# Moving the maxima's subtraction, delta*x and the values' products in a planned attention, routing and scan kernel

## The chip, the cores and the metric

One core of one Trainium2 chip runs the whole kernel. The time is device microseconds for one execution, the median of the runs shown; a profiled execution, taken apart from these, gives the trace.

## The reference, cut to what matters

Sixteen independent sequences of 512 tokens and 256 features (B, T, D = 16, 512, 256) in float32 pass through four blocks. Each block adds its result to x.

```python
def attn_a(x):                       # on layernorm(x)
    xn = x * rsqrt(mean(x * x) + EPS) * norm_w
    q, k, v = heads(xn @ Wq.T + bq), heads(xn @ Wk.T + bk), heads(xn @ Wv.T + bv)   # 16 heads of 16
    scores = where(causal, -inf, q @ k.T / 4)
    out = softmax(scores) @ v
    return xn + out @ Wo.T + bo

def attn_b(x):                       # selective scan with 16 states, on layernorm(x)
    xc = silu(conv4(x) + conv_b)
    delta = softplus(xc @ Wd.T + bd)
    Bm, Cm = xc @ Wb.T, xc @ Wc.T
    h = exp(A * delta) * h + delta * xc * Bm     # for each feature and state, step by step over T
    y = sum_over_states(h * Cm)
    return (y * sigmoid(x @ Wg.T + bg)) @ Wo.T + bo

def ffn(x):                          # base product, a shared low rank and 2 of 6 routed low ranks
    return base(x) + shared(x) + sum(top2_weight * routed(x))

x = x + attn_a(layernorm(x)); x = x + ffn(layernorm(x))
x = x + attn_b(layernorm(x)); x = x + ffn(layernorm(x))
```

## The kernel before, in words

**The plan.** The loop over the 16 sequences (L886) doesn't issue instructions. It records operations with `op(engine, cost, function, r=, w=, ...)` (L84): an engine, an estimated duration, the buffers read and written, and further buffers that have to be free at its start (`also`). `Plan.order` (L126) then plays the whole list through a small model of the engines: at each moment a free engine takes, among its ready operations whose buffers are free, the one with the smallest due time. The due time is `STARTS[sequence] + TURNS[place in the sequence]` (L130), two tables of numbers written out in the file. For ScalarE, `CHANGE` is added to the due time of an operation that needs another activation table than the loaded one (L149). While a score product waits for its reader, `kept` reserves the reader's engine (and TensorE afterwards), so that a filler is taken only if it ends at most `OVER` after the reserved moment (L151 to L154). The order that comes out is the order of the instructions in each engine's queue, and an engine works its queue in order; the waits on the chip are real semaphores, so a wrong estimate can only make an engine stand still. For a DMA, the model takes its issue (0.65 or 0.7 us), then a share of one common link (`load`, 2.3 us for a scan load) and 2.0 us until it has landed.

**Buffers.** `sizes` (L415) gives the number of each: 4 of x (so at most four sequences are under way), 3 of qT, 4 of kT, 2 of qm, one each of pt0 to pt3, 5 of dd. In PSUM there are one buffer `sc` of four banks for scores and four single banks `one`.

**Attention** (L538). Tokens are normalised and transposed into xtA. Heads come in four groups j of four; two groups make a pair i. For a pair one product gives the queries of 8 heads, each in 16 of 128 rows; two ScalarE passes (L626) write it to two tiles qT, in each of which every second block of 16 rows is scaled to zero, so that each head of a group has a block of 32 rows of which 16 are zero. kT is made in the same way, with a 1 in the first row of the zero half (bk with first_row added). Then:

- for each query tile t of 128 tokens and each group, `four` (L560) runs four score products (one per head, 32 rows of the array each, L566) and four products with identb and a mask (full array, L568) into sc, and VectorE takes the negated row maximum (L637) into negm;
- negm is transposed on TensorE (L645); the maximum of a head then lies in the first of the zero rows of that head;
- VectorE adds this row to the queries: qm = one * first_row + qT (L650), one for each group of the pair. With the 1 in kT, the score product then contains the maximum's subtraction;
- `weights_values` (L575): for each key tile kt, `four` gives the transposed scores in sc, ScalarE exponentiates them into pt (L585), and four products `weigh` (L590; tiles of 128 rows and 32 columns, one per head) accumulate values and the row sum over kt in one bank. Each of the four weigh steps is an operation of its own. The sums are copied (L596), transposed (L601) and divided (L608, L609).

Then the heads' outputs are transposed and projected (L662 to L671).

**Scan** (L766). After convolution and gates, delta (dt, L812) and delta*x (dx, which takes a buffer of tag sg, L817, on VectorE) are stored to DRAM in rows (L816, L819), and read back with each row spread over 16 partitions (dd, L849, two DMAs of 512 KB for each of 16 dd tiles of a sequence). GpSimd multiplies by B (L856), ScalarE makes the decays in a bank (L861), VectorE scans (L864), GpSimd multiplies by C (L867), and TensorE sums over the states with ysel (L874, again tiles of 128 rows and 32 columns). All DMAs of a sequence are issued by SyncE, in planned order. In the model, operations with `port=True` (GpSimd's and L817) exclude each other.

**Routing** (L674) is run after attention and after the scan: low-rank products (L687), the top two of six by small VectorE operations, one transposition (L754) and the projection.

`project` (L515) ends each block: products into a bank, then VectorE adds it to x (L528).

## Time and profile before

| | |
|---|---|
| median of 3 runs | 2063.27 us (2061.38 to 2065.82) |
| the profiled execution's own time | 2066.51 us |
| its span, first to last instruction | 2064.7 us |
| mean granted TensorE clock | 0.954 |
| instructions | 34733 |
| scans, L864 on DVE | 512 x 1212 ns |
| products by B and C, L856 and L867 on POOL | 256 x 2361 and 256 x 2358 ns |
| row maxima, L637 on DVE | 256 x 1486 ns (684 to 2285) |
| exponentials, L585 on ACT | 256 x 1235 ns (594 to 1872) |
| moved by DMA | 316 MB, 153 GB/s over the span |

How to read it. The page gives the busy time of each engine, then 40 slices of the span with a digit for tenths of busy time. A group line has the line of the code, the engine, the operation, output and inputs, shapes and count; then busy time and mean of one; then the idle time of the engine just ahead of it and what ended it. In a timeline a line is a run of like instructions: start, duration, engine, line, operation, and in brackets a wait ahead of it. A float32 product counts as two TensorE instructions, so that a step of four products appears as x8. Ends of products are modelled and overlap the next start. PEld is the load of weights. The x16 of the DMA issues to L889 and L894 are the loads and stores of the 16 sequences.

### The profile page before, as it was taken

Reading aid. Unit: us, or ns where it says so; the run is one execution under the profiler, and the core shown is the slowest. Engines: PE = TensorE matmul, PEld = TensorE weight load, DVE = VectorE, ACT = ScalarE, POOL = GpSimd, SP = SyncE. Lnnn points to the kernel's source line nnn. Section 1 sums busy time; section 2 is a strip of 40 time slices with the busy share of each in tenths; the row PEclk is TensorE's granted clock in tenths of the full one; section 3 lists DMA queues with packets and bytes.
Section 4 is the critical chain, followed back from the end, with each engine's and each line's share of the span. In section 5 each row is a group of like instructions: output and inputs, shape, how many; then the busy total and the mean of one; then the engine's idle time right before and its main releaser. Section 6 shows DMA issues by size and latency. Waiting matters only on the chain. (4 is left out here: it accounts for less than half of the span.)

```text
span 2064.7 us, 34733 instructions
## 1 busy us (share of the span) xinstructions
PE 1801.9 (87%) x13253; PEld 953.8 (46%) x13253; DVE 1513.4 (73%) x2479; ACT 1194.0 (58%) x1685; POOL 1371.1 (66%) x814
## 2 busy tenths in 40 slices
PE   4788789999999999999999999999999999996455
PEld 2244344555455454545455454545554454544123
DVE  4335677878788787878788787878788787876563
ACT  2236556565666757565666667575666766564431
POOL 3001784949587685859597785859596785848693
PEclk8789899999999999999999999999999999998766
DMA  3000956848494866847494867849493957747791
GB/s 93 1 1 22 216 122 155 197 127 210 109 233 109 216 164 167 205 137 191 110 231 100 225 153 175 204 120 212 110 231 95 228 143 186 183 125 183 186 222 31
DMA packets 113064, 316.35 MB, mean 153 GB/s; under 512 B 17809, under 2 KB 36610, under 8 KB 112898
## 3 DMA queue, kind: packets, MB, share of 16 engines
q1 hardware_dynamic: 112194, 313.99, 62.5%
q8 instruction: 105, 1.72, 0.4%
q14 instruction: 61, 0.50, 0.1%
q10 hardware_dynamic: 704, 0.14, 0.0%
HBM read 287.87 MB, written 26.21 MB: 152 GB/s over the span
## 5 line engine op out<-in xcount | busy, mean ns | idle before, releaser
L864 DVE TENSOR_TENSOR_SCAN dd<-one,dd 128x512 f32<-128x512 f32 x512 | 607.9, 1212 | 185.2 <-ACT one L861 88.3
L856 POOL TENSOR_TENSOR dd<-dd,bc 128x1024 f32<-128x1024 f32 x256 | 603.6, 2361 | 194.0 <-DMA dd<-drows 156.8
L867 POOL TENSOR_TENSOR dd<-dd,bc 128x1024 f32<-128x1024 f32 x256 | 601.9, 2358 | 86.2 <-DVE dd L864 80.4
L637 DVE TENSOR_REDUCE negm<-sc 128x4 f32<-128x512 f32 (+3 forms) x256 | 380.4, 1486 | 154.0 <-PE sc L568 153.7
L861 ACT ACTIVATE one<-dd,am 128x512 f32<-128x512 f32 x512 | 344.3, 689 | 249.4 <-DVE dd L864 108.9
L585 ACT ACTIVATE pt<-sc 128x2048 f32<-128x2048 f32 (+3 forms) x256 | 316.3, 1235 | 189.0 <-PE sc L568 187.8
L487 POOL TENSOR_SCALAR rs<-mv 128x4 f32<-128x4 f32 x64 | 12.3, 193 | 364.2 <-DVE mv L482 361.4
L566 PE MATMUL sc<-qm,kT 32*128 32x512 f32 (+3 forms) x2048 | 214.1, 488 | 37.8 <-ACT pt L585 28.4
L566 PE MATMUL sc<-kT,qT 32*128 32x128 f32 (+3 forms) x2048 | 217.0, 494 | 30.5 <-DVE negm L637 25.9
L568 PEld LDWEIGHTS <-identb 128*128 128x128 bf16 x2048 | 117.4, 98 | 232.4 <-issue 217.2
L874 PE MATMUL one<-dd,ysel 128*32 128x512 f32 x1024 | 172.7, 633 | 55.5 <-POOL dd L867 46.4
L590 PE MATMUL one<-pt,vv 128*32 128x512 f32 (+3 forms) x2048 | 191.6, 449 | 8.1 <-DVE dd L864 7.9
L566 PEld LDWEIGHTS sc<-qm,kT 32*128 32x128 f32 x2048 | 80.9, 185 | 181.5 <-ACT pt L585 120.4
L474 PE MATMUL one<-base,xtR 128*128 128x256 f32 x512 | 139.5, 395 | 18.6 <-DVE dd L864 18.0
L566 PEld LDWEIGHTS sc<-kT,qT 32*128 32x128 f32 x2048 | 82.0, 187 | 156.8 <-DVE negm L637 63.3
L494 ACT ACTIVATE xhR<-x,nm,rs 128x256 f32<-128x256 f32 x192 | 99.4, 588 | 53.2 <-POOL nm L490 53.1
L528 DVE TENSOR_TENSOR x<-one,x 128x512 f32<-128x512 f32 x128 | 86.4, 675 | 34.7 <-PE one L474 34.5
L474 PEld LDWEIGHTS one<-base,xtR 128*128 128x128 f32 x512 | 94.5, 194 | 36.8 <-DVE dd L864 21.5
L481 DVE BATCH_NORM_STATS2 st<-x 128x6 f32<-128x256 f32 x256 | 103.7, 405 | 4.8 <-DMA x<-in_x_dram 4.1
L568 PE MATMUL sc<-mask_q,identb 128*128 128x128 bf16 x1024 | 103.7, 225 | 0.0
L568 PE MATMUL sc<-mask_k,identb 128*128 128x128 bf16 x1024 | 102.8, 224 | 0.0
L505 PE MATMUL one<-ident,xhR 128*128 128x128 f32 x384 | 61.9, 290 | 35.2 <-ACT xhR L494 27.7
(132 smaller groups left out, 2449.4 us busy)
## 6 DMA issues: line engine op xcount, KB each, us to landing
dd<-drows SPq DMA_DIRECT2D x512, 512.0 KB
x<-in_x_dram SPq DMA_DIRECT2D x16, 512.0 KB
drows<-dt SPq DMA_DIRECT2D x32, 256.0 KB
drows<-sg SPq DMA_DIRECT2D x32, 256.0 KB
bc<-brows SPq DMA_DIRECT2D x16, 512.0 KB
out_dram<-x SPq DMA_DIRECT2D x16, 512.0 KB
brows<-few SPq DMA_DIRECT2D x16, 64.0 KB
wo<-in_Wo_dram SPq DMA_DIRECT2D x2, 256.0 KB
```

The source lines that it names most:

```text
L474: nc.tensor.matmul(o[:, lo:hi], lhsT=lhsT, rhs=rhs, start=n == 0, stop=n == len(todo) - 1)
L481: nc.vector.bn_stats(st()[:, t, :], x()[:, t, :])
L566: nc.tensor.matmul(sc()[:, g, 0:n], lhsT=lhsT(g), rhs=rhs(g), start=True, stop=False)
L568: nc.tensor.matmul(sc()[:, g, at : at + P], lhsT=identb, rhs=mask, start=False, stop=True)
L585: o.then = op("ACT", act(G * n), lambda pt=pt, sc=sc, n=n: nc.scalar.activation(pt(), sc()[:, :, 0:n], AF.Exp), r=[sc], w=[pt], table="exp")
L590: nc.tensor.matmul(av()[rows(g), kt * P : T], lhsT=vals()[:, kt, G * j + g, :], rhs=pt()[:, g, :], start=kt == 0, stop=kt == NT - 1,)
L637: o.then = op("DVE", dve(G * n), lambda t=t, n=n, sc=sc, nm=nm, s=s: nc.vector.tensor_reduce(nm()[:, t, :, 1 - s, 0:1], sc()[:, :, 0:n], A ...
L856: op("POOL", pool(1024), lambda dd=dd: nc.gpsimd.tensor_tensor(dd()[:, :, 1, :], dd()[:, :, 1, :], both(0), ALU.mult), port=True, r=[(bc, ...
L861: op("ACT", act(512) + 0.07, lambda i=i, k=k, dd=dd, dec=dec: nc.scalar.activation(dec(), dd()[:, i, 0, :], AF.Exp, scale=am[:, k + 4 * i ...
L864: op("DVE", 1.22, lambda i=i, dd=dd, dec=dec: nc.vector.tensor_tensor_scan(dd()[:, i, 1, :], dec(), dd()[:, i, 1, :], 0.0, ALU.mult, ALU.a ...
L867: op("POOL", pool(1024), lambda dd=dd: nc.gpsimd.tensor_tensor(dd()[:, :, 1, :], dd()[:, :, 1, :], both(1), ALU.mult), port=True, r=[(bc, ...
L874: nc.tensor.matmul(sums()[rows(g), :], lhsT=ysel[:, m, :], rhs=four[g]()[:, g % 2, 1, :], start=m == 0, stop=m == 3)
```

## The change

- The row maxima: the transposed negm is copied by ScalarE to a new tile nT (one buffer), and for each group of the pair one DMA on SyncE's queue copies its four rows (2 KB each) from nT into the first zero rows of qT, in place. The two VectorE operations into qm and the qm buffers are gone; qT has 4 buffers in place of 3, and stays in use until the last score product of its group.
- `weigh` is one operation for each group, behind its four exponentials: 16 products in one run, four key tiles one after the other. It reads pt0 to pt3 and is marked `mode="columns"`, as L874's sum is; in the model an operation of TensorE costs 0.2 us less behind one of the same mode.
- delta*x is computed by GpSimd in place of VectorE.
- The plan: estimates of several operations, OVER, CHANGE and both tables of due times have new values; a sequence has 366 operations in place of 376.

```diff
-OVER, CHANGE = 2.3, 97.0
+OVER, CHANGE = 2.5, 0.0
 STARTS = (
-    0, 149, 234, 338, 413, 521, 619, 700, 790, 888, 996, 1074, 1174, 1263, 1369, 1447,
+    0, 332, 605, 865, 1160, 1414, 1634, 1884, 2099, 2343, 2583, 2879, 3172, 3456, 3728, 3999,
 )
...
+                if eng == "PE":
+                    cost -= 0.2 * (o.mode is not None and o.mode == mode)
+                    mode = o.mode
...
-        "hT": (2, [NU + 1, T]), "qT": (3, [P, T]), "kT": (4, [P, T]), "qm": (2, [P, T]), "avs": (2, [P, T]),
+        "hT": (2, [NU + 1, T]), "qT": (4, [P, T]), "kT": (4, [P, T]), "nT": (1, [P, T]), "avs": (2, [P, T]),
...
     def act(n):
-        return 0.2 + n / 1200.0
+        return 0.17 + n / 1200.0
...
-            o = op("PE", pe(n, 1, 0.09) + 0.45, run, r=reads, w=[sc], also=[into])
+            o = op("PE", pe(n, 1, 0.0) + 0.5, run, r=reads, w=[sc], also=[into])
...
             av, avs = psum("one"), sbuf("avs")
+            pts = [sbuf(f"pt{kt}") for kt in range(NT)]
             for kt in range(NT):
                 n = T - kt * P
-                pt = sbuf(f"pt{kt}")
+                pt = pts[kt]
...
-                def weigh(kt=kt, pt=pt, av=av, j=j):
+            def weigh():
+                for kt in range(NT):
                     for g in range(G):
                         nc.tensor.matmul(
-                            av()[rows(g), kt * P : T], lhsT=vals()[:, kt, G * j + g, :], rhs=pt()[:, g, :],
+                            av()[rows(g), kt * P : T], lhsT=vals()[:, kt, G * j + g, :], rhs=pts[kt]()[:, g, :],
                             start=kt == 0, stop=kt == NT - 1,
                         )
 
-                op("PE", pe(n, 1, 0.1), weigh, r=[pt, vals], w=[av], also=[avs])
+            op("PE", 2.2 + 0.2, weigh, r=pts + [vals], w=[av], also=[avs], mode="columns")
...
-            qms = [sbuf("qm"), sbuf("qm")]
-            op("PE", 0.66, turn, r=[nm], w=[one], also=qms)
-            for s, qm in enumerate(qms):
-                op("DVE", dve(512) + 0.06, lambda qm=qm, one=one, qT=pairs[s][0], s=s: nc.vector.scalar_tensor_tensor(
-                    qm(), one(), first_row[:, 1 - s : 2 - s], qT(), ALU.mult, ALU.add
-                ), r=[one, pairs[s][0]], w=[qm])
-            for s in range(2):
-                weights_values(2 * i + s, pairs[s][1], qms[s])
+            nT = sbuf("nT")
+            op("PE", 0.57, turn, r=[nm], w=[one], also=[nT])
+            op("ACT", act(512), lambda nT=nT, one=one: nc.scalar.copy(nT(), one()), r=[one], w=[nT])
+            for s, (qT, kT) in enumerate(pairs):
+                row = slice(HD * (1 - s), P, 32)
+                op("SP", 0.65, lambda nT=nT, qT=qT, row=row: nc.sync.dma_start(out=qT()[row, :], in_=nT()[row, :]),
+                   r=[nT], w=[qT], load=0.1)
+            for s, (qT, kT) in enumerate(pairs):
+                weights_values(2 * i + s, kT, qT)
...
-            op("DVE", dve(512) + 0.1, lambda e=e: nc.vector.tensor_tensor(dx()[:, e, :], dt()[:, e, :], xc()[:, e, :], ALU.mult),
+            op("POOL", pool(512), lambda e=e: nc.gpsimd.tensor_tensor(dx()[:, e, :], dt()[:, e, :], xc()[:, e, :], ALU.mult),
                r=[(dt, e), (xc, e)], w=[(dx, e)], port=True)
...
-                op("PE", pe(512, 1, 0.18), add, r=[four[0], four[2]], w=[sums])
+                op("PE", pe(512, 1, 0.18), add, r=[four[0], four[2]], w=[sums], mode="columns")
```

The due times (TURNS) are replaced throughout and left out here. Other estimates that change: a step of four transpositions 0.66 to 0.57, the division 0.72 to 0.68, the routing's small VectorE steps by 0.08 to 0.2 each, the values' products less 0.2.

## The prediction

> **What bounds the kernel now.** I read five views: the busy shares and slices of the page, the stretches, SyncE's timeline (for the rhythm), TensorE's timeline (for what one step costs there), and the groups by shape (for durations).
>
> ```profile
> PE 1801.9 (87%) x13253; PEld 953.8 (46%) x13253; DVE 1513.4 (73%) x2479; ACT 1194.0 (58%) x1685; POOL 1371.1 (66%) x814
> PE   4788789999999999999999999999999999996455
> ```
>
> ```profile
> 155.00:1858.00 1703.00, 1584.71 (x12054) 841.64 (x12056) 1347.02 (x2182) 1077.01 (x1518) 1208.48 (x702) 0.99 0.67 164
> 1858.00:2064.00 206.00, 111.70 (x468) 60.09 (x468) 112.61 (x184) 71.75 (x110) 145.45 (x77) 0.73 0.66 156
> ```
>
> The columns after the length are PE, PEld, DVE, ACT and POOL busy, then PE's clock and the DMA share. PE is at 9 tenths in nearly every slice between a head and a tail: 93% from 155 to 1858 us, 54% in the last 206 us. In the middle DVE has 79%, POOL 71%, ACT 63% and the DMA engines 67%. PE's own timeline lists 112 us of waits in that stretch, 6.6%. So the middle is PE's, taken in order; the tail is latency, with POOL the busiest.
>
> SyncE's timeline (start, duration) gives the rhythm:
>
> ```profile
> 1092.38 0.54 SPq L894 DMA_DIRECT2D out_dram<-x  x1
> 1102.95 0.39 SPq L889 DMA_DIRECT2D x<-in_x_dram  x1
> 1207.93 0.55 SPq L894 DMA_DIRECT2D out_dram<-x  x1
> 1219.17 0.38 SPq L889 DMA_DIRECT2D x<-in_x_dram  x1
> 1323.70 0.55 SPq L894 DMA_DIRECT2D out_dram<-x  x1
> ```
>
> The first sequence is stored at 399.8 us, then one every 115.5 us until 1785.8 (12 periods, 1386 us), then three in the last 275 us. A period holds 115.5 x 0.066 = 7.6 us of PE waits and 107.9 us of PE work.
>
> What does a weighting step (L590) cost on PE? Its timeline tells if starts are compared:
>
> ```profile
> 998.27 0.50 PE L566 MATMUL sc<-qm,kT 32*128 32x128 f32 x8
> 998.71 0.40 PE L568 MATMUL sc<-mask_k,identb 128*128 128x128 bf16 x4
> 999.04 1.07 PE L590 MATMUL one<-pt,vv 128*32 128x512 f32 x8
> 1000.03 0.71 PE L566 MATMUL sc<-qm,kT 32*128 32x256 f32 x8
> 1000.68 0.40 PE L568 MATMUL sc<-mask_k,identb 128*128 128x128 bf16 x4
> 1001.01 0.85 PE L590 MATMUL one<-pt,vv 128*32 128x384 f32 x8
> 1001.68 1.04 PE L874 MATMUL one<-dd,ysel 128*32 128x512 f32 x8
> 1002.65 0.50 PE L566 MATMUL sc<-kT,qT 32*128 32x128 f32 x8
> 1003.08 0.40 PE L568 MATMUL sc<-mask_q,identb 128*128 128x128 bf16 x4
> 1003.41 0.64 PE L590 MATMUL one<-pt,vv 128*32 128x256 f32 x8
> 1003.98 0.66 PE L601 MATMUL one<-ident,avs 128*128 128x128 f32 x4
> ```
>
> Modelled ends overlap, so I take start to next start. The 384-wide step before L874, also in 128x32 tiles, takes 0.67 us; its others before a full-array product take 0.78 (median). The 256-wide one takes 0.46 before L874, 0.57 before a full-array product (here), 0.76 before scores. With no change of tile shape I get 0.25, 0.46, 0.67 and 0.88 us for 128 to 512 columns (the 0.25 and 0.88 by the 0.21 per 128 columns): 2.26 us for four. Leaving column tiles adds 0.11 to 0.30. Entering them adds 0.10: the four mask products last 0.33 us before L590 and 0.23 before a full-array product, over 300 cases.
>
> **What the Trainium skill says.** "TensorEngine Tiling (Array Packing)", section Tiling Modes, says that changing the tiling mode drains TensorE; the 0.10 and 0.11 to 0.30 us above agree. "DMA: Bandwidth & Descriptors", section Why a DMA increments its semaphore by 16 and not by 1, says that a transfer runs on the largest number of engines up to 16 that divides its slowest dimension, the lowest-numbered ones: the new transfers have 4 rows, so 4 engines, on the queue that carries the scan's loads. No such shape is in the trace. "SBUF — State Buffer", section Who interferes with whom, says that a VectorE operation with two SBUF inputs and a GpSimd one exclude each other; L817 (two SBUF inputs) takes 809 ns, the same shape from PSUM (L880) 685, which fits. "ScalarE: Activation LUTs", What ACT_TABLE_LOAD costs, gives 1283 ns; the trace has 1283, 68 times.
>
> **The change, part by part.**
>
> ```profile
> L650 DVE SCALAR_TENSOR_TENSOR qm<-one,first_row,qT 128x512 f32<-128x512 f32 x64 | 44.8, 741 | 12.4 <-PE one L645 12.4
> L817 DVE TENSOR_TENSOR sg<-dt,xc 128x512 f32<-128x512 f32 x32 | 25.9, 809 | 8.6 <-ACT dt L812 8.6
> L856 POOL TENSOR_TENSOR dd<-dd,bc 128x1024 f32<-128x1024 f32 x256 | 603.6, 2361 | 194.0 <-DMA dd<-drows 156.8
> ```
>
> 1. Values' products in one run. Between 155 and 1858 us there are 222 steps, 4 to a group of heads. About half are followed by scores, a third by full-array products, 39 by L874 (no change). Weighted with the medians (0.12 after 512 and 384 before scores, 0.30 after 256, 0.11 before full arrays) the exits come to 27.9 us, 0.50 per group of heads; 221 of 222 are entered from a full array, 0.10 each, 0.40 per group. One run pays one exit (0.11 to 0.30) and one entry: 0.25 to 0.40 in place of 0.90, so 0.50 to 0.65 us less; I take 0.65. Four groups: **2.6 us of PE per period**, 41.6 us over 64 groups. Against it: four score weights (pt0 to pt3, one buffer each) stay taken until the run is over, so the next group's first score product waits for about 2.3 us more. The score buffer sc is held per group for 8.7 us of PE (3.02 of scores and 1.32 of masks, twice), 10.9 us of reductions and exponentials and some 3 us of handing over, 22.5 of the 28.9 us that a quarter period has: 6.4 us are spare. I take zero; if that cover is gone it costs up to 2.3 x 4 = 9.2 us a period.
>
> 2. Maxima by ScalarE and transfers. Removed: 64 of L650, 44.8 us of DVE, 3.0 a period. Added: 32 ScalarE copies like L596 (583 ns), 18.7 us, on an engine with 63%; 64 SyncE issues at 0.33 us (the issue of the small store L829), 21 us; 64 transfers of 8 KB, little beside 512 KB each for the scan. Path from the transposed maxima to the first score product: before 2 x 0.74 = 1.5 us on DVE for both heads; after 0.58 + 2 x 0.33 + a landing. Nearest for the landing: from the store of few (1021.02) to the load that waits for it (1022.74), 1.7 us. So 2.9 us in place of 1.5: 1.4 later, twice a period, hidden where PE has products of three other sequences in between. Upper end: behind ten of the scan's loads at 2.16 us each (62.5% of the span over some 600 loads' worth of bytes), 21.6 us. Lower end: below nothing, since DVE's own queue no longer delays it. I take zero. Behind a waiting transfer on SyncE stand the scan's loads, for which POOL L856 waits; behind a waiting score product stands all of PE.
>
> 3. Delta*x on GpSimd. DVE loses 25.9 us, 1.6 a period. POOL gains 32 at half of L856 plus something, 1.2 us: 38 us, 2.4 a period, on 71%. Each of the two is 0.4 us later for its store, and may stand behind one 2.36 us product; POOL is mostly idle there, since the scan has not begun. Zero.
>
> 4. Order. Costs, due times (STARTS, TURNS), OVER and CHANGE all change, so every queue is laid out anew. CHANGE 0 takes away the preference for the loaded ScalarE table: between none and 8 more loads of 1.28 us a period (six activations alone among exponentials would need 12 where 4.25 are now). The trace bounds this to 0 to 10 us of ScalarE a period; I take zero, as ScalarE has 37% free.
>
> Sum: 12 periods x 2.6 = 31 us; of the other 16 groups (head and tail, PE half busy) half of 16 x 0.65, 5 us. PE waits behind the scan on DVE for 43 us in the middle (L474, L645, L505, L590 by L864); with 4.6 of 91 us less on DVE I count nothing. The profiled run is 2066.5 us (span 2064.7 and 1.8 around it): 2066.5 - 36 = 2030.5. It lies 3.2 above the median of the runs, so **2027 us**, 1.7% faster. Next late is still PE, with 112.9 a period.
>
> **Rivals.**
> More gain: the waits of 43 us behind DVE's scan go too, and POOL and DVE no longer exclude each other at delta*x: 2027 - 43 = 1984. For it: DVE is second at 79%. Against: those waits are for PSUM buffers, not for DVE's load.
> No gain: an x buffer comes free only with a store, and the next load follows it by 10 us; if the 450 us that a sequence stays set the period, PE's gain is idle time: 2063. Against: a sequence's own chain (attention 90 us of sc, scan 75 us of POOL) is much shorter.
> **Slower**: the small transfers arrive later than the fixed order of PE assumes. The place is the first score product of a pair of head groups, twice a period; PE stops there with all that is queued behind. It decides from 1.3 us of lateness each (2 x 1.3 = 2.6). Behind one or two of the scan's loads, 3 us each, it costs 12 x (6 - 2.6) = 41 us: 2104. With the pt buffers' 9.2 us a period in full it would be 12 x 6.6 = 79: 2142. For it: SyncE's queue is in order, and it waits 715 us in all for scan buffers to come free (dd by L874). Against: the order counts 2 us and the load of the link for each transfer.
> That it doesn't do what it says: the runs of four may stand where a switch is needed anyway, and the due times may undo the rest; 2060.
>
> **How the numbers follow.** Forecast 0.40 (2005 to 2055, own range), more gain 0.15, no gain 0.08, slower 0.35, not as said 0.02. About 0.2% (4 us) is what a measurement of this kernel can tell from no change. Faster: 0.40 + 0.15 + 0.03 of the two weak cases; same 0.07; slower 0.35. The range leaves out some 0.07 of the strong gain below 1988 and 0.13 of the losses above 2100.
>
> **What would show it.** Right: a store every 112 to 113 us, L590 some 10% shorter in sum, PE above 92% in the middle. Wrong: PE waiting at L566 for a transfer into qT, waits at sc for pt, table loads far above 68, DMA waits at L856 grown, or a longer tail.

## The result and the profile after

| | before | after |
|---|---|---|
| median of the runs made side by side | 2064.55 us (4 runs) | 2146.77 us (2144.03 to 2156.54, 4 runs) |
| ratio, 95% interval | | 1.0409 (1.0372 to 1.0446) |
| the profiled execution | 2066.51 us | 2144.24 us |
| its span | 2064.7 us | 2142.4 us |
| mean granted TensorE clock | 0.954 | 0.918 |

The kernel became slower, by 82 us where 36 us less was forecast, and it lies above the range. In the page of the kernel after, these are TensorE's busy share and its slices, with the granted clock in tenths:

```profile
PE 1827.1 (85%) x13253; PEld 982.5 (46%) x13253; DVE 1445.5 (67%) x2383; ACT 1208.2 (56%) x1719; POOL 1410.8 (66%) x846
...
PE   5778789998989989899989999899989999987445
...
PEclk8679899999999999999999999999999999988657
```

TensorE has the same 13253 products and is busy for 25 us longer, although one run of the values' products was to save time. SyncE's timeline of the kernel after, with the stores (L903) and loads (L898) of x:

```profile
984.00 0.39 SPq L903 DMA_DIRECT2D out_dram<-x  x1
988.70 0.39 SPq L898 DMA_DIRECT2D x<-in_x_dram  x1
...
1103.47 0.39 SPq L903 DMA_DIRECT2D out_dram<-x  x1
1107.58 0.54 SPq L898 DMA_DIRECT2D x<-in_x_dram  x1
```

A store comes every 119.5 us here, in place of 115.5; over 12 periods the mean is 119.8. The load of B and C for the scan (bc), one for each sequence, gives a cleaner sum of the 78 us: the first comes at 222 us in place of 205 (+17), the 15 intervals after it have 119.6 in place of 115.8 (+57), and from the last to the end there are 126.7 us in place of 122.2 (+4). So most of the loss, 57 of the 78 us, is in the rhythm. The first scan's later start was not looked into.

What TensorE waits for, of the kernel before (total us, times, longest):

```profile
PE one L874 <- POOL dd L867: 46.4, 28, 7.2
PE sc L566 <- ACT pt L585: 32.7, 83, 2.0
PE one L505 <- ACT xhR L494: 27.7, 7, 10.7
PE sc L566 <- DVE negm L637: 26.3, 22, 2.4
```

and of the kernel after:

```profile
PE sc L570 <- ACT pt L590: 115.1, 101, 3.3
PE one L883 <- POOL dd L876: 65.5, 36, 12.0
PE sc L570 <- DVE negm L644: 45.1, 46, 3.7
```

The wait of a score product for the exponentials that read the score buffer before it has grown by 82 us. That this is as much as the loss is chance: the period has 4.3 us of it (below), beside other changes. No line of TensorE's products has a transfer into qT. To see where that wait stands, TensorE's timeline of the kernel after:

```profile
959.44 0.93 PE L570 MATMUL sc<-qT,kT 32*128 32x384 f32 x8
960.30 0.40 PE L572 MATMUL sc<-mask_k,identb 128*128 128x128 bf16 x4
962.23 0.50 PE L570 MATMUL sc<-qT,kT 32*128 32x128 f32 x8 [1.54 <-ACT pt L590]
962.67 0.40 PE L572 MATMUL sc<-mask_k,identb 128*128 128x128 bf16 x4
963.75 1.24 PE L570 MATMUL sc<-qT,kT 32*128 32x256 f32 x8 [0.69 <-ACT pt L590]
964.92 0.61 PE L572 MATMUL sc<-mask_k,identb 128*128 128x128 bf16 x4
966.64 2.09 PE L570 MATMUL sc<-kT,qT 32*128 32x512 f32 x8 [1.11 <-ACT pt L590]
968.66 0.61 PE L572 MATMUL sc<-mask_q,identb 128*128 128x128 bf16 x4
969.20 3.00 PE L597 MATMUL one<-pt,vv 128*32 128x512 f32 x32
```

Four score steps follow one another with nothing but waits between them, and the run of 32 (L597, the values' products) stands behind all four. In the timeline of the kernel before, the weigh steps and other products stand between such steps. The durations tell a second thing: from 963.75 on the score step of 256 columns takes 1.24 us, the one of 512 takes 2.09, where the prediction's lines have 0.71 for 256, and 1.14 (at 955.99 in the kernel after) is normal for 512. The stretches of the kernel after (PEclk is the third figure from the end) say why:

```profile
957.00:964.00 7.00, 4.62 (x52) 3.38 (x52) 4.04 (x13) 6.02 (x8) 3.93 (x2) 0.98 1.04 233
964.00:971.00 7.00, 5.89 (x36) 1.99 (x40) 5.45 (x12) 3.30 (x5) 7.00 (x4) 0.53 1.05 233
971.00:1077.00 106.00, 99.41 (x759) 54.63 (x752) 80.16 (x123) 66.00 (x97) 76.96 (x48) 1.00 0.64 156
```

After a stretch in which TensorE was busy for 4.6 of 7 us, its clock is halved for some 7 us, once a period; the same happens at 844 us. In the kernel before no record between 303 and 1883 us has a lowered clock. The Trainium skill, "TensorE: Matmul & The Clock Gate", section A second HAM failure mode: psum-queue depth-cycling, says that frequent short idle times between groups of products can make the clock go back and forth between half and full; this trace agrees, with waits of at most 1.54 us in the stretch ahead.

To compare kernels below, I add up TensorE's timeline between the stores of the first and the thirteenth sequence, by start to next start less the waits, and divide by 12. "Work" is all of it, "weigh" the values' products, "for pt" the waits of a score product for exponentials; "half clock" is the time for which the clock records have half speed there.

| us a period | period | work | of it weigh | waits | of them for pt | half clock |
|---|---|---|---|---|---|---|
| before | 115.5 | 109.1 | 11.4 | 6.3 | 1.4 | 0 |
| after | 119.8 | 109.9 | 10.0 | 9.9 | 5.7 | 7.7 |

### The profile page after: what moved, and what is told of

Its sections match the earlier page's. It is cut to its first block, busy times and chain, and to the rows that moved or that the text cites. A ratio compares the mean times of both kernels' runs of the same rounds, so it can differ in the third digit from the quotient of the medians.

```text
span 2142.4 us, 34874 instructions
## 1 busy us (share of the span) xinstructions
PE 1827.1 (85%) x13253; PEld 982.5 (46%) x13253; DVE 1445.5 (67%) x2383; ACT 1208.2 (56%) x1719; POOL 1410.8 (66%) x846
## 4 chain that ended last, share of the span: by engine, by line
PE 55%; POOL 13%; DVE 12%; ACT 10%; issue 4%; DMA 4%; SPq 0%; POOLq 0%; ACTq 0%; DVEq 0%
PE one L478 21%; PE sc L570 13%; PE one L597 7%; POOL dd L876 6%; PE sc L572 6%; ACT pt L590 5%; PE one L883 4%; DVE dd L873 4%; DMA dd<-drows 4%; DVE negm L644 3%; POOL dd L865 3%; POOL rs L492 2%; ACT xhR L498 2%; PE one L509 1%; DVE st L485 1%
## 5 line engine op out<-in xcount | busy, mean ns | idle before, releaser
L644 DVE TENSOR_REDUCE negm<-sc 128x4 f32<-128x1024 f32 (+3 forms) x256 | 380.1, 1485 | 235.5 <-PE sc L572 233.2
L590 ACT ACTIVATE pt<-sc 128x512 f32<-128x512 f32 (+3 forms) x256 | 316.5, 1236 | 196.0 <-PE sc L572 195.0
L570 PE MATMUL sc<-qT,kT 32*128 32x512 f32 (+3 forms) x2048 | 223.3, 507 | 100.4 <-ACT pt L590 85.5
L570 PE MATMUL sc<-kT,qT 32*128 32x256 f32 (+3 forms) x2048 | 232.4, 525 | 61.6 <-DVE negm L644 31.9
L572 PEld LDWEIGHTS <-identb 128*128 128x128 bf16 x2048 | 122.0, 101 | 249.5 <-issue 234.9
L826 POOL TENSOR_TENSOR sg<-dt,xc 128x512 f32<-128x512 f32 x32 | 40.5, 1266 | 204.3 <-ACT dt L821 204.3
L597 PE MATMUL one<-pt,vv 128*32 128x512 f32 (+3 forms) x2048 | 171.5, 480 | 0.3 <-DVE dd L873 0.2
L491 POOL TENSOR_SCALAR rs<-mv 128x4 f32<-128x4 f32 x64 | 12.3, 193 | 236.9 <-DVE mv L486 233.1
L570 PEld LDWEIGHTS sc<-qT,kT 32*128 32x128 f32 x2048 | 84.8, 194 | 176.4 <-ACT pt L590 108.9
L597 PEld LDWEIGHTS one<-pt,vv 128*32 128x32 f32 x2048 | 63.6, 118 | 100.7 <-issue 84.0
L572 PE MATMUL sc<-mask_k,identb 128*128 128x128 bf16 x1024 | 107.6, 231 | 0.0
```

Of the source, the lines that this page charges most:

```text
L570: nc.tensor.matmul(sc()[:, g, 0:n], lhsT=lhsT(g), rhs=rhs(g), start=True, stop=False)
L572: nc.tensor.matmul(sc()[:, g, at : at + P], lhsT=identb, rhs=mask, start=False, stop=True)
L590: o.then = op("ACT", act(G * n), lambda pt=pt, sc=sc, n=n: nc.scalar.activation(pt(), sc()[:, :, 0:n], AF.Exp), r=[sc], w=[pt], table="exp")
L597: nc.tensor.matmul(av()[rows(g), kt * P : T], lhsT=vals()[:, kt, G * j + g, :], rhs=pts[kt]()[:, g, :], start=kt == 0, stop=kt == NT - 1,)
L644: o.then = op("DVE", dve(G * n), lambda t=t, n=n, sc=sc, nm=nm, s=s: nc.vector.tensor_reduce(nm()[:, t, :, 1 - s, 0:1], sc()[:, :, 0:n], A ...
```

## The experiments

Two families: in the first the order of the instructions is that which the kernel before has (its plan is made as it was, and only what is emitted differs), so that a part is tried without the new due times; in the second it is that of the changed kernel.

**The parts one at a time, in the order of before**

*weigh_run*: the weigh steps of a group are held back and emitted in one run at the last one's place (earlier where another group's exponentials need the same pt).

```diff
...
+            if o.key is not None:
+                held.append((*o.key, o.fn))
+                if o.key[1] < NT - 1:
+                    continue
+                mine = [h for h in held if h[0] is o.key[0]]
+                held = [h for h in held if h[0] is not o.key[0]]
+                for _, _, fn in mine:
+                    fn()
+                continue
```

> The kernel before with its own planned order, and one edit: the four weighting steps of a group are held back and issued together where the last of them stood. All other instructions keep their places in every queue. Theory of the cover (the weighting steps were what TensorE did while ScalarE exponentiates; held back, they leave the scores bare, and the idle stretch also drops the clock to half): of the 2.0 us that move out of the holes of a group, about half finds no other filler, so 4 us of new waits a period against 2.6 us of tile changes saved, and 2 to 3 us a period lost at half clock: about 2110 us, at least 2085, with more waits of the score products for pt. Theory of the order (the run saves what I forecast, and the new due times lose it elsewhere): 12 x 2.6 = 31 us less, about 2032 us.

*max_dma*: the ScalarE copy to nT and SyncE's two transfers stand where the two VectorE operations stood. qT has 6 buffers here.

```diff
...
-                op("DVE", dve(512) + 0.06, lambda qm=qm, one=one, qT=pairs[s][0], s=s: nc.vector.scalar_tensor_tensor(
-                    qm(), one(), first_row[:, 1 - s : 2 - s], qT(), ALU.mult, ALU.add
-                ), r=[one, pairs[s][0]], w=[qm])
+                def rows_in(qm=qm, one=one, qT=pairs[s][0], s=s, nTs=nTs):
+                    if not nTs:
+                        nTs.append(sb.tile([P, T], F32, tag="nT", name="nT", bufs=1))
+                        nc.scalar.copy(nTs[0], one())
+                    row = slice(HD * (1 - s), P, 32)
+                    nc.sync.dma_start(out=qT()[row, :], in_=nTs[0][row, :])
+                    qm.tile = qT()
+                op("DVE", dve(512) + 0.06, rows_in, r=[one, pairs[s][0]], w=[qm])
```

> The kernel before with its own planned order, and one edit: in place of the two VectorE operations into qm, ScalarE copies the transposed maxima to nT and two transfers on SyncE's queue write their rows into qT (6 buffers of qT, so that none is waited for). Theory of the transfer (my rival: late rows stop TensorE at the first score product of a pair): over 2085 us, with waits of TensorE there. Theories of the cover and of the order: within 10 us of 2064.

*dx_pool*: delta*x on GpSimd.

```diff
-            op("DVE", dve(512) + 0.1, lambda e=e: nc.vector.tensor_tensor(dx()[:, e, :], dt()[:, e, :], xc()[:, e, :], ALU.mult),
+            op("DVE", dve(512) + 0.1, lambda e=e: nc.gpsimd.tensor_tensor(dx()[:, e, :], dt()[:, e, :], xc()[:, e, :], ALU.mult),
```

> The kernel before with its own planned order, and one edit: delta*x on GpSimd. All theories: within 6 us of 2064, since GpSimd has little to do there; more than 10 us slower would be a cause of its own, GpSimd standing at delta*x with the scan's products behind it.

*all_three*: the three edits together.

> The three edits together in the planned order of the kernel before: the operations of the changed kernel without its new due times. Theory of the cover: about as the run of four alone, 2110 us. Theory of the order: 2027 us, so that the whole loss and more lies in the new order. Theory of the transfer: over 2100 us.

| | median us | ratio (95%) | against its before |
|---|---|---|---|
| weigh_run | 2182.2 | 1.0585 (1.0559 to 1.0610) | +119 |
| max_dma | 2329.5 | 1.1302 (1.1277 to 1.1328) | +266 |
| dx_pool | 2064.6 | 1.0003 (0.9993 to 1.0012) | +1 |
| all_three | 2455.6 | 1.1905 (1.1885 to 1.1924) | +392 |

So the two parts whose cover the prediction took as complete cost 119 and 266 us without a new order, and all but add up (119 + 266 + 1 = 386 against 392). The new order (due times, estimates, OVER and CHANGE together, with 4 buffers of qT) then takes back 310 of the 392 us. Whether that order also costs something of its own is not shown, since the operations of the kernel before were not laid out in it. In weigh_run and max_dma TensorE waits for these above all; a fence for each:

```profile
PE sc L567 <- ACT pt L586: 129.4, 148, 2.0
```

```profile
PE sc L568 <- DMA qT<-nT: 245.4, 32, 18.7
```

The second is the prediction's slower rival, in kind and in place: 32 waits, one for each pair of head groups, of 7.7 us on average. Is it the transfer or SyncE's queue?

*max_actq*: max_dma with `nc.scalar.dma_start` in place of `nc.sync.dma_start`.

> The kernel before with its own planned order and the maxima by copy and transfers, as in max_dma, but issued by ScalarE. If the 266 us of max_dma come from SyncE's queue, in which the transfers stood behind waiting scan loads: below 2120 us. If they come from the transfer's own time and from the scan's data that fill the same engines: 2250 or more.

2206.2 us, 1.0687 (1.0655 to 1.0718), +143: the queue is worth some 120 us. The wait for qT that stays is 122 us. The ScalarE timeline and then TensorE's show one late transfer:

```profile
1104.87 0.60 ACT L656 COPY nT<-one 128x512 f32<-128x512 f32 x1
1106.35 2.59 ACTq L658 DMA_DIRECT2D qT<-nT  x2
```

```profile
1105.03 1.82 PE L476 MATMUL one<-low,xtR 128*128 128x118 f32 x14 [0.17 <-ACT xtR L510]
1112.85 2.09 PE L568 MATMUL sc<-qT,kT 32*128 32x512 f32 x8 [6.00 <-DMA qT<-nT]
```

It is issued at 1106.35 us, on a queue without scan loads, and TensorE goes on at 1112.85, 6.5 us later. Ten loads of 512 KB for the scan are issued by SyncE from 1094.7 to 1110.4 us. The pair of head groups before it, on the same queue, goes otherwise:

```profile
1043.88 0.51 ACTq L658 DMA_DIRECT2D qT<-nT  x1
```

```profile
1045.67 1.14 PE L568 MATMUL sc<-qT,kT 32*128 32x512 f32 x8 [0.76 <-DMA qT<-nT]
```

Here TensorE goes on 1.8 us after the issue. The 32 pairs fall into two halves: in 16 TensorE goes on 1.8 to 1.9 us after the issue, and the DMA engines move 8 to 16 GB/s in the 2 us after it; in the other 16 it goes on after 6.4 to 7.5 us, and they move 234 to 333 GB/s. These 16 hold some 105 of the 122 us of waits. So the transfer itself is short, and it is late where the scan's loads are moving. The Trainium skill, "DMA: Bandwidth & Descriptors", section Issuing engines are not separate DMA queues, says that transfers of all issuing engines run on the same 16 DMA engines and interleave; that agrees, and fits that another queue takes away only a part.

**How the held steps cost 119 us**

In weigh_run the period is 123.2 us (before 115.5), with 7.6 us of waits for pt (before 1.4) and 13.1 us of half clock (before 0), and the weigh steps take 10.5 in place of 11.4. The stretches from the first to the thirteenth store, of before and of weigh_run:

```profile
400.00:1786.00 1386.00, 1305.36 (x9938) 697.25 (x9937) 1123.40 (x1825) 889.27 (x1261) 1025.44 (x601) 1.00 0.70 170
```

```profile
422.00:1900.00 1478.00, 1328.94 (x9938) 723.45 (x9936) 1123.93 (x1825) 888.33 (x1261) 1026.80 (x602) 0.95 0.66 159
```

*weigh_fill2*: weigh_run with 12 small products, which nothing reads, in each place that a held step left.

```diff
                 if o.key[1] < NT - 1:
+                    for _ in range(12 * (o.key[0] not in begun)):
+                        nc.tensor.matmul(o.key[0]()[:, 0:P], lhsT=identb, rhs=mask_k, start=True, stop=True)
                     continue
```

> weigh_run (the kernel before, each group's weighting steps held back to the last one's place), and in each emptied place 12 small bf16 products (identity by mask, 128 columns, about 0.7 us, into the bank that the run overwrites later). They compute nothing that is used. In weigh_run the clock is at half for 13 us a period and scores and masks take 3.0 us a period more than before. If the half clock is a cause of its own: no half clock, 2 to 4 us a period less, 2120 to 2150. If it only shows the waits and costs nothing itself: 2182 within 10.

2120.3 us, 1.0264 (1.0249 to 1.0280). Added work made weigh_run 62 us faster, as the theory of a clock with a cost of its own has it (2120 to 2150). Its stretch from first to thirteenth store has full clock again (third figure from the end):

```profile
410.00:1835.00 1425.00, 1363.36 (x11667) 803.26 (x11664) 1125.63 (x1825) 890.17 (x1261) 1027.01 (x602) 1.00 0.68 165
```

The sum of a period, by the same adding up: the added products take 9.6 us, the waits fall by 7.4 (12.3 to 4.8), and the other products take 6.6 us less, as much as 13.1 us at half clock lose. So the added products fill waits for the most part, take some 2 us beyond them, and pay for that with the clock. At least 62 of the 119 us are the clock that a bare stretch takes away. That the rest is the waits which the weigh steps used to fill is argued from the waits for pt, not shown by an edit.

*weigh_pairs* and *weigh_last*: the edit of weigh_run, with two runs of two, and with only the third step held to the fourth.

```diff
-                if o.key[1] < NT - 1:
+                if o.key[1] % 2 == 0:
...
-                if o.key[1] < NT - 1:
+                if o.key[1] == NT - 2:
```

> The kernel before with its own planned order; the first weighting step of a group is held back to the second's place and the third to the fourth's: two runs of two. Half as many steps are moved out of the holes as in weigh_run (0.88 + 0.46 of the 2.0 us) and half of the tile changes are saved. Theory of the cover: about half of the loss of weigh_run or less, 2090 to 2125. Theory that any run of steps saves: below 2055.

> The kernel before with its own planned order; only the third weighting step (256 columns, 0.46 us) is held back to the fourth's place. One exit and one entry are saved for each group, 0.2 to 0.4 us, 13 to 26 us in all; one small step leaves a hole, which the steps of 512 and 384 columns did not. Theory of the cover: the loss depends on what else stands in that hole; from -15 us (covered by other work) to +25 (bare): 2050 to 2090.

2082.3 us, 1.0085 (1.0071 to 1.0098), and 2065.1 us, 1.0003 (0.9993 to 1.0013). Work on TensorE falls to 107.3 and 108.0 us a period, which is the saving that was meant, but waits for pt rise to 5.2 and 2.7 us. In weigh_last it comes out even: 1.1 us less work, 1.2 us more waits, the same 115.5 us.

**In the order of the changed kernel**

*after_split*: where a bank is free for it (37 of 64 groups), the run is taken apart again: a weigh step that is ready follows the next score step; what is left comes at the run's place.

```diff
...
+            if o.exp:
+                ready.append(o.exp)
+            if o.four:
+                for av, kt in [r for r in ready if r[0] in early]:
+                    if left[av] > 1:
+                        left[av] -= 1
+                        parts[av](kt, False)
+                        ready.remove((av, kt))
```

> The changed kernel with its own planned order, and one edit: in the 37 of 64 groups where a bank is free for it from the first exponential on, the weighting steps are taken out of the run again, each behind the next score step after its exponential, all but the last, which stays. All other instructions keep their places. Theory of the cover: two of four groups of a period are split, the one that stands bare among them; waits for pt fall by 3 us a period and the half clock of 2 to 3 us goes, against 1.3 us more for tile changes: 119.8 to about 116 us a period, 2100 us (2085 to 2120). Theory that the new due times alone lose: 12 x 1.3 = 16 us more, about 2160.

*after_dve_max*: the two VectorE operations, in place into qT, stand where the copy to nT was; no transfer.

```diff
-            op("ACT", act(512), lambda nT=nT, one=one: nc.scalar.copy(nT(), one()), r=[one], w=[nT])
+            def rows_in(one=one, pairs=pairs):
+                for s, (qT, kT) in enumerate(pairs):
+                    nc.vector.scalar_tensor_tensor(qT(), one(), first_row[:, 1 - s : 2 - s], qT(), ALU.mult, ALU.add)
+            op("ACT", act(512), rows_in, r=[one], w=[nT])
...
```

> The changed kernel with its own planned order, but where ScalarE copied the maxima, VectorE adds them to both qT in place; no copy, no transfers. The trace of the changed kernel has no wait of TensorE for the transfers, so the theory of the cover expects 2147 within 12. Theory that the transfers cost in their new places too (SyncE stands 272 us before them, with the scan's loads behind): 2110 or less.

*after_actq*: the transfers are issued by ScalarE (`nc.scalar.dma_start` in place of `nc.sync.dma_start`, nothing else).

> The changed kernel with its own planned order, but the transfers of the maxima are issued by ScalarE right after its copy, so that SyncE's queue never stands before them. If SyncE's standing holds back scan loads that matter: 2110 to 2135. If not: 2147 within 12, or slower by ScalarE's two issues, 64 times.

| | median us | ratio (95%) | period | waits for pt | for negm | half clock |
|---|---|---|---|---|---|---|
| after | 2146.8 | 1.0409 (1.0372 to 1.0446) | 119.8 | 5.7 | 1.3 | 7.7 |
| after_split | 2134.3 | 1.0352 (1.0330 to 1.0374) | 120.2 | 3.7 | 4.1 | 1.7 |
| after_dve_max | 2181.9 | 1.0581 (1.0565 to 1.0597) | 122.8 | 6.2 | 0.9 | 12.2 |
| after_actq | 2145.9 | 1.0401 (1.0378 to 1.0424) | 119.8 | 5.8 | 1.3 | 8.3 |

In its own order the changed kernel has no use for VectorE's maxima (they cost 35 us more there, which neither theory expected) and none for another queue of transfers. Taking the run apart gives 12 us, between the two theories of that run. The period does not get shorter: the gain is ahead of the first store, which comes at 375.1 us in place of 386.2. It doesn't get shorter although half clock falls from 7.7 to 1.7 us a period, without added products. The waits turned, as TensorE's waits of after_split show:

```profile
PE sc L571 <- DVE negm L645: 90.4, 81, 3.7
PE sc L571 <- ACT pt L592: 69.6, 77, 3.3
```

Less waiting for pt than after's 115.1, twice the waiting for negm, which had 45.1.

*after_fill*: the changed kernel's run stays whole, and 12 small products stand in the places where after_split had a step.

```diff
                     if left[av] > 1:
                         left[av] -= 1
-                        parts[av](kt, False)
+                        for _ in range(12):
+                            nc.tensor.matmul(av()[:, 0:P], lhsT=identb, rhs=mask_k, start=True, stop=True)
                         ready.remove((av, kt))
```

> The changed kernel with its own planned order; in the same places where after_split issued weighting steps early (37 groups), 12 small bf16 products are issued instead, and the run of four stays whole. They compute nothing that is used. after_split took 12 us off. If that was the clock: as much or more here, 2115 to 2138. If it was the weighting work moved into the holes: 2147 to 2160.

2150.8 us, 1.0404 (1.0385 to 1.0423). Half clock falls from 7.7 to 1.1 us a period and the time does not. But the added products take 4.8 us a period, while waits fall by 1.2 and the other products by 2.4, so this run alone doesn't say what the clock costs here. Together with after_split, whose period stays with the clock mended, it says that mending the clock is not enough in this order, in contrast to weigh_run.

**A theory that fell: GpSimd's scan sets the rhythm.** By GpSimd's own timeline a scan takes 88.7 us and the gap to the next 27 us in a period of before, and 92.8 and 27 after; two bias additions lie inside the scan after, and outside it before. If GpSimd were the bound, taking those away would give their time back.

*after_no_bias* and *before_no_bias*: the bias additions are left out. *scales_lean*: before, with small operations of a normalisation moved to VectorE. *p1_dve*: before, with some products by B moved to VectorE.

```diff
-        op("POOL", pool(1024), lambda: nc.gpsimd.tensor_tensor(
-            x(), x(), bias.unsqueeze(1).to_broadcast([P, NT, D]), ALU.add
-        ), port=True, w=[(x, t) for t in range(NT)])
+        op("POOL", pool(1024), lambda: None, port=True, w=[(x, t) for t in range(NT)])
...
-            nc.gpsimd.tensor_scalar(rs()[:, :, 0], mv()[:, :, 1], eps, 1.0, ALU.add, ALU.mult)
+            nc.vector.tensor_scalar(rs()[:, :, 0], mv()[:, :, 1], eps, 1.0, ALU.add, ALU.mult)
+            nc.vector.tensor_scalar(nm()[:, :, 0], mv()[:, :, 0], -1.0, 0.0, ALU.mult, ALU.add)
...
-            nc.gpsimd.tensor_scalar(nm()[:, :, 0], mv()[:, :, 0], -1.0, 0.0, ALU.mult, ALU.add)
...
-                    op("POOL", pool(1024), lambda dd=dd: nc.gpsimd.tensor_tensor(
+                    op("POOL", pool(1024), lambda dd=dd, m=m, g=g: (nc.vector if (m, g) == (2, 0) else nc.gpsimd).tensor_tensor(
```

> The changed kernel with its own planned order, without the two additions of a bias to x on GpSimd (bo and bo2 are left out of the result; each is one 128x1024 operation of 2.36 us for a sequence). Theory of the scan (the period is GpSimd's scan plus a fixed gap, and these two stand inside the scan): 4.7 us a period less, 15 periods, 2147 - 70 = about 2077. Theory that TensorE's bare exponentials and its clock set the period: 2147 within 12.

> The kernel before with its own planned order, without the same two additions (bo and bo2 are left out of the result). There they stand in the gap behind the last product of a scan, where GpSimd then waits 13 us for something else. Theory of the scan: 2064 within 8. A loss of 20 us or more would say that GpSimd's total work counts, wherever it stands.

> The kernel before with its own planned order; of the four small GpSimd operations of a normalisation, the two that only read the variance and the mean go to VectorE, at the same place. Three of four normalisations of a period stand inside the scan, at 0.28 + 0.28 us each. Theory of the scan: 3 x 0.56 = 1.7 us a period, 25 us less, 2039 (2030 to 2050). Theory that TensorE bounds the kernel: 2064 within 8.

> The kernel before with its own planned order; 2 of the 16 products by B of a scan (L856) go to VectorE, at the same place, 2.36 us less on GpSimd each and about 1.2 us more on VectorE. Theory of the scan: up to 4.7 us a period less, 2064 - 70 = 1994, if VectorE keeps up (to 2030 if its scans come later by half of it). Theory that TensorE bounds the kernel (109 us of work in 115.5): 2064 within 8, or slower by VectorE's load.

after_no_bias 2152.6 us (1.0423, 1.0408 to 1.0439), before_no_bias 2064.6 (1.0001, 0.9991 to 1.0011), scales_lean 2064.5 (0.9998, 0.9987 to 1.0010), p1_dve 2079.3 (1.0077, 1.0055 to 1.0099). Nothing became faster. In after_no_bias GpSimd is busy for 80.2 us of a scan in place of 84.7, and idle in it for 11.9 in place of 8.1: it follows the others.

**The last two.** *split_actq*: after_split with the transfers issued by ScalarE. *tail_fill*: before, with small products that nothing reads in the last sequence's scan.

```diff
-                op("SP", 0.65, lambda nT=nT, qT=qT, row=row: nc.sync.dma_start(out=qT()[row, :], in_=nT()[row, :]),
+                op("SP", 0.65, lambda nT=nT, qT=qT, row=row: nc.scalar.dma_start(out=qT()[row, :], in_=nT()[row, :]),
...
+            if o.fill and o.seq == B - 1 and o.num > last_exp:
+                if spare is None:
+                    spare = ps.tile([P, G, 512], F32, tag="sc", name="sc", bufs=1)
+                for _ in range(o.fill):
+                    nc.tensor.matmul(spare[:, 0, 0:P], lhsT=identb, rhs=mask_k, start=True, stop=True)
```

> The changed kernel's order, the weigh steps taken out of their run where a bank is free, and the transfers of the maxima issued by ScalarE instead of SyncE. Theory that the two waits share the period (each covers for the other when one is taken away): about 2095 to 2115 us, the period of 120 us down to about 118, and the waits for negm of the run with the split alone (4.07 us a period) mostly gone. Rival, that the loss lies in the order in which the changed kernel's steps are laid and not in either wait: 2134 us as with the split alone, within 6 us, the waits for negm as they were.

> The kernel before, with small bf16 products that nothing reads added on TensorE between the steps of the last sequence's scan, after the last exponential, into a bank that is free by then. Theory that the slow clock of the tail costs time (its products of that stretch run at half clock while TensorE mostly waits): 6 to 9 us less than the kernel before, ratio 0.996 to 0.997. Rival, that the tail is paced by GpSimd and VectorE and not by TensorE's clock: no change, within 3 us.

split_actq: 2125.0 us, 1.0309 (1.0294 to 1.0324). That is some 9 us below after_split, where after_actq alone had 1, and between the two theories. The period is still 119.6 us, and waits for pt and negm are still 3.8 and 3.9 us. So the loss of the rhythm goes neither with one of the two edits nor with both; what the 9 us are was not found.

tail_fill: 2063.8 us, 1.0010 (1.0001 to 1.0018). The last stretch of before and of tail_fill:

```profile
1940.00:2064.00 124.00, 60.56 (x212) 31.89 (x212) 56.41 (x99) 28.38 (x47) 79.62 (x42) 0.67 0.59 140
```

```profile
1940.00:2062.00 122.00, 73.09 (x512) 47.38 (x512) 56.56 (x99) 28.44 (x48) 80.10 (x42) 0.78 0.60 145
```

The clock rose from 0.67 to 0.78 and nothing was gained: no time of the tail was found to hang on TensorE's speed. No run beat the kernel before; weigh_last, scales_lean and dx_pool equal it.

## Why the prediction was wrong, point by point

**The bound.** That TensorE sets the middle held in one sense only. It works its queue in order and is busy for 94% of it, but weigh_last takes 1.1 us of work a period from it without any gain. What sets the rhythm is the queue together with the engines that it waits for; a saving counts only if no wait takes its place.

**Part 1, the values' products: here the prediction failed.** "I take zero; if that cover is gone it costs up to 2.3 x 4 = 9.2 us a period." The zero is the step that failed, and the cost has another place than the one named. The text looked for the cost behind the run, at the next group's first score product, since pt0 to pt3 stay taken until the run is over. Little of it stands there: of the 129 us of waits for pt in weigh_run 21 fall on the first two score steps behind a run, of the 115 us in the kernel after 3. The rest stands ahead of the run, between the score steps of a group.

The cover was worked out from the time that the score buffer is held, an average over a quarter period. What counts is what TensorE does in each short gap while ScalarE exponentiates out of the one score buffer. That was the weigh steps: three of them a group are 0.88 + 0.67 + 0.46 = 2.0 us, 8 us a period, and of these 6.2 came back as waits for pt in weigh_run (7.6 less 1.4).

The price in weigh_run, 7.7 us a period, is near the upper end that the text had, but that is luck: it comes from another place, and in part from the clock, which is not in the text at all. The emptied stretch of scores is followed by half clock, at least 62 us of weigh_run's 119. In the kernel after the same signs stand, 4.3 us a period more waits for pt and 7.7 us of half clock; how much of its 82 us they are is not shown, since taking 37 of the 64 runs apart gave 12.

The saving itself exists: 1.4 us a period for weigh in the kernel after, where runs stand at half clock, and 2.4 in weigh_fill2, where the clock is full, against 2.6 forecast. The groups agree in sum, first of before, then of after:

```profile
L590 PE MATMUL one<-pt,vv 128*32 128x512 f32 (+3 forms) x2048 | 191.6, 449 | 8.1 <-DVE dd L864 7.9 <-ACT pt L585 0.2
```

```profile
L597 PE MATMUL one<-pt,vv 128*32 128x512 f32 (+3 forms) x2048 | 171.5, 480 | 0.3 <-DVE dd L873 0.2
```

20 us less, the "some 10%" that was to be seen, and yet no gain.

**Part 2, the transfers.** "I take zero" was wrong in the old order by 266 us, of which 143 stay when SyncE's queue is out of it. In the changed kernel it was right: only weight loads of TensorE wait there for qT, 0.9 us in all, and after_actq changes nothing. Its order asks for the transfers early enough. The landing was bounded from 1.7 to 21.6 us; in max_actq TensorE went on after 1.8 us in half of the cases, the estimate but for 0.1, and after 6.4 to 7.5 in the other half. The longest wait in max_dma was 18.7.

**Part 3, delta*x.** Zero, as forecast (dx_pool, +1 us, within its interval of 0). The operation costs 1.27 us (1.2 in the text):

```profile
L826 POOL TENSOR_TENSOR sg<-dt,xc 128x512 f32<-128x512 f32 x32 | 40.5, 1266 | 204.3 <-ACT dt L821 204.3
```

**Part 4, the order.** It was taken as zero without a sum, but for the table loads, and it is worth 310 us against the parts' 392. The fear of more table loads did not come true in number (70 in place of 68), but in place: the line that loads the exponential's table once a sequence is now L590, the exponentials of attention, in place of the scan's decays:

```profile
L590 ACT ACT_TABLE_LOAD x15 | 19.2, 1283 | 6.8 <-PE sc L572 6.5
```

It stands ahead of the bare stretch. The chain of waits of the kernel after, in order of time (start, duration, what), passes through it in every period:

```profile
950.71 1.02 POOL rs L492
952.30 2.08 ACT xhR L498 x4
...
956.21 1.28 ACT L590
957.51 1.88 ACT pt L590
...
966.64 2.09 PE sc L570 x8
969.27 2.94 PE one L597 x32
...
1070.10 1.02 POOL rs L492
1071.69 2.08 ACT xhR L498 x4
...
1075.61 1.28 ACT L590
1076.91 1.88 ACT pt L590
```

The same piece comes back after 119.4 us, the period: a normalisation on GpSimd, ScalarE's passes, the table, the exponentials that TensorE waits for, the slow run, and then pieces of all engines until the next sequence's normalisation. What this doesn't say is which link could be shortened with a gain.

**The rivals.** "Slower" named late transfers (2104 us) and the pt buffers in full, 12 x (9.2 - 2.6), which gave 2142 us. The transfers are not late in the kernel after. The second sum is near the 2146.8 measured, and its kind of wait is the one that grew, but not by 9.2 us a period: waits for pt grew by 4.3, the halved clock is not in that sum, and of the 78 us only 57 are in the rhythm. So the number is close by luck.

**What stays open.** Why the period keeps to about 120 us in the changed kernel's order when the run is taken apart (which mends the clock too), when the bare places are filled, or when the run is taken apart and the transfers have another queue: with the run taken apart, waits for pt become waits for negm. That this order contains a ring over several engines, as the chain has it, fits, but was not shown by an edit that breaks it. The table load inside the ring was not moved. The rival that the new order has a cost of its own, whatever the operations, stands untested: the operations of the kernel before were not laid out in it.

## What to carry to other kernels

Before work is moved to another place in a queue that is taken in order, look at what it fills: here a product that stood in another engine's shadow was free where it was, and its place became a wait when it was gone. Try each part alone in the old order, so that the parts' own costs and the new order's repair are seen apart. A small saving on the busiest engine is worth something only if the wait behind it doesn't grow by as much; read the waits along with the work, and the clock along with both.

## What the runs showed of the hardware

- In the kernel after, a stretch of 7 us in which TensorE was busy for 4.6, with waits of 1.54 and 0.69 us between score steps, was followed by some 7 us at half clock. Products that nothing reads, put in the gaps of weigh_run, made it 62 us faster (half clock 13.1 to 0 us a period). In the changed kernel (7.7 to 1.1) and in the tail (clock 0.67 to 0.78) they gave nothing.
- A transfer of 4 rows of 2 KB within SBUF, issued from a queue without loads (max_actq), let TensorE go on 1.8 us after its issue when the DMA engines moved 8 to 16 GB/s just after it, and 6.4 to 7.5 us after it when loads of 512 KB on another queue made that 234 to 333 GB/s.
- Two issues of such a transfer took 1.22 us on SyncE's queue in the kernel after (0.56 each by the median of 64), where the prediction had 0.33 from a small store.
